# Cross-attention and a mixture of experts: how layer-normed tokens are transposed in front of the experts

## The chip, the cores and the metric

The kernel runs on one core of a Trainium2 chip. The metric is the device time of one execution in microseconds, lower is better. The kernel before takes 726.56 us (median of 3 runs, 726.43 to 727.07).

## The reference

All in f32. 1600 tokens (16 batches of 100) of width 256 pass a cross-attention over 361 context rows each and then a feed-forward stage with one shared and seven switched experts:

```python
def xattn(x, y, Wq, Wkv, Wproj, bproj):            # 16 heads of 64
    q = heads(x @ Wq); k, v = heads(y @ Wkv)
    a = softmax(q @ k.T * 64 ** -0.5) @ v
    return merge(a) @ Wproj + bproj

def swiglu(h, w1, w2, w3):                          # 256 -> 704 -> 256
    return silu(h @ w1.T) * (h @ w3.T) @ w2.T

def ffn(x, ...):
    probs = sigmoid(clip(x @ router_w.T + routing_bias, -50, 50))
    p, sel = top_k(probs, 1)
    y = swiglu of expert sel, times p
    total = clip(0.5 + p + 1e-8, 0.5, 2.0)
    return 0.5 / total * swiglu(x, shared) + y / total

x = x + xattn(layernorm(x), ctx, ...)
x = x + ffn(layernorm(x), ...)
```

## The kernel before

Tokens lie in 13 tiles of 128 (the last has 64). `acc` holds the residual stream, 128 tokens of a tile on the partitions; `xT` holds the normalised tokens turned round, features on the partitions (two halves of 128, index k), tokens along the free dimension, for use as the moving operand of TensorE. Four `GROUPS` of tiles, (0-2), (3-5), (6-8), (9-12), are handled together.

**Attention loop.** 32 steps `s`, two per batch (eight heads each). In each step, TensorE computes scores (L628) in pairs of heads, and between them the next key or value products (L561). VectorE finds the row maxima (L641), ScalarE takes exponentials (L644), and VectorE transposes the result in blocks of 32 into `tb` (L657). `moved` (L668) then puts the blocks in their places with 16 transfers into `aT`, eight issued by SP and eight by GpSimd, after a small transfer `row` and before two transfers `over` on SP. At the even steps `values` (L690) multiplies aT of the batch before with its values (L699). Two `tb` and two `aT` exist, so each is written again two steps on.

**Layer norm.** `layer_norm` (L161) returns a list of parts, `moments` per tile, `roots`, `normalise` per tile, and `turn`, which transposes the normalised tiles `xn` on TensorE against an identity, two tiles into one PSUM bank (L203), and copies the bank to `xT` on ScalarE (L206). With `keep=True` it is the norm in front of the experts: `normalise` also writes `xn` to DRAM (`xn_d`, L192), from where the experts gather tokens. The same function without `keep` is the norm in front of the attention. In the loop, `normalised` (L735) puts the parts into a queue `norms`, of which `part()` takes one behind most score units; once they are used up, `turned` is queued and runs at the next even step, and after it the router (`router`, L226, whose products at L235 read `xT`). So groups 0, 1 and 2 are normalised for the experts about steps 10 to 14, 18 to 22 and 26 to 30.

**Loads.** `load_later` (L150) issues, at the end of a step, what later steps need. Steps 10 to 15 call `load_shared` (L214): 10 to 13 load the four parts of the shared expert's first weights `w13_sb`, 14 the first three of the six row blocks of `w2_sb` (L220), 15 the other three by two transfers (L223, L224).

**Behind the loop.** The last step already computes the first hidden units of the shared expert for group 0 (`hidden`, L403, products at L412). Then come `down(GROUPS[0][:2])`, the first use of `w2_sb` (products at L455), the values of the last batch, `down` of the group's third tile, and the last projections (L726), which complete `acc`. Then:

```python
parts, turn_last = layer_norm(GROUPS[-1], keep=True)
for one in parts: one()
hT = run_hidden(GROUPS[1])
turn_last()
down(GROUPS[1][:1], hT)
for one in router(GROUPS[-1]): one()
down(GROUPS[1][1:], hT[:, :, P:])
fill = sort_tokens(hs)
```

`sort_tokens` gives the expert of each of up to 19 slots of 128 tokens; `fetch` (L881) has SP load an expert's weights by that number, and `gather_into` (L897) has GpSimd gather tokens. The other hidden and down products of the shared expert and then the slots follow.

**Order.** TensorE's order is the order of the text in the whole kernel. In the attention part, up to the last projection, the same holds for ScalarE, VectorE and SP; a scheduler places GpSimd's instructions, and behind the attention those of all engines but TensorE. Each DMA queue issues in its own order, and an issue that waits holds up those behind it. Waits between engines are semaphores that the framework puts in where tiles overlap.

Of the kernel before, what the change touches and what calls it, by code (L numbers as in the profile page):

```python
# [14 lines left out]
F32 = mybir.dt.float32  # L15
# [7 lines left out]
B, LQ, C = 16, 100, 256  # L23
# [3 lines left out]
P = 128  # L27
N = B * LQ
NT = (N + P - 1) // P
LAST = N - (NT - 1) * P  # L30
# [10 lines left out]
GROUPS = ((0, 1, 2), (3, 4, 5), (6, 7, 8), (9, 10, 11, 12))  # L41
# [13 lines left out]
def xattn_moe(  # L55
# [16 lines left out]
    nc = tc.nc  # L72

    def rows(t):
        return P if t < NT - 1 else LAST
# [9 lines left out]
    xT = const.tile([P, 2, NT * P], F32, name="xT")  # L85
# [24 lines left out]
    w2_sb = const.tile([P, NI + 1, C], F32, name="w2_sb")  # L110
# [4 lines left out]
    def bank():  # L115
        return ps.tile([P, 512], F32, tag="mm", name="mm")
# [10 lines left out]
    def load_x(g):  # L127
        full = [t for t in g if t < NT - 1]
        t0, n = full[0], len(full)
        nc.sync.dma_start(  # L130
            acc[:, t0 : t0 + n, :],
            x[t0 * P : (t0 + n) * P, :].rearrange("(t p) c -> p t c", p=P),
        )
        if g[-1] == NT - 1:
            nc.sync.dma_start(acc[:LAST, NT - 1, :], x[(NT - 1) * P :, :])
# [22 lines left out]

    biases = deque()

    def layer_norm(tiles, keep=False):  # L161


        n = len(tiles)
        of, xns = {}, []

        def moments(i):
            if i == 0:
                of["mv"] = small.tile([P, 4, 2], F32, name="mv")
                of["rstd"] = small.tile([P, 4], F32, name="rstd")  # L170
            st = small.tile([P, 6], F32, name="st")
            nc.vector.bn_stats(st, acc[:, tiles[i], :])
            nc.vector.bn_aggr(of["mv"][:, i, :], st)

        def roots():
            rstd = of["rstd"]
            nc.vector.tensor_scalar(rstd[:, :n], of["mv"][:, :n, 1], EPS, None, ALU.add)
            nc.gpsimd.tensor_tensor(rstd[:, :n], rstd[:, :n], power[:, :n], ALU.pow)

        def normalise(i):  # L180
            t = tiles[i]
            xn = small.tile([P, C], F32, name="xn", bufs=4)
            nc.vector.tensor_scalar(
                xn,
                acc[:, t, :],
                of["mv"][:, i, 0:1],
                of["rstd"][:, i : i + 1],
                ALU.subtract,
                ALU.mult,
            )  # L190
            if keep:
                nc.sync.dma_start(xn_d[t * P : t * P + rows(t), :], xn[: rows(t), :])  # L192
            else:
                biases.append(t)
            xns.append(xn)

        def turn():
            for i in range(0, n, 2):
                tr = bank()
                m = min(2, n - i)  # L200
                for o in range(m):
                    for k in range(2):
                        nc.tensor.transpose(  # L203
                            tr[:, ds((k * m + o) * P, P)], xns[i + o][:, ts(k, P)], ident
                        )
                nc.scalar.copy(  # L206
                    xT[:, :, ds(tiles[i] * P, m * P)],
                    tr[:, : 2 * m * P].rearrange("p (k n) -> p k n", k=2),
                )

        parts = [lambda i=i: moments(i) for i in range(n)] + [roots]
        return parts + [lambda i=i: normalise(i) for i in range(n)], turn

    def load_shared(i):  # L214

        if i < 4:
            k, o = i // 2, ds(i % 2 * I, I)
            nc.sync.dma_start(w13_sb[:, k, o], w13[ts(k, P), o])
        elif i == 4:
            nc.sync.dma_start(w2_sb[:, :3, :], w2[: 3 * P].rearrange("(i p) c -> p i c", p=P))  # L220
        else:
            r = w2[3 * P : NI * P].rearrange("(i p) c -> p i c", p=P)
            nc.sync.dma_start(w2_sb[:, 3:NI, :], r)  # L223
            nc.sync.dma_start(w2_sb[P - HALF :, NI, :], w2[NI * P :])  # L224
# [178 lines left out]
    def hidden(g, hT, sp, width=NB, same_table=0):  # L403


        n = sum(map(rows, g))

        nc.gpsimd.memset(hT[: P - HALF, NI, :n], 0.0)

        def product(to, at):  # L410
            for k in range(2):
                nc.tensor.matmul(  # L412
                    to[:, :n],
                    w13_sb[:, k, ds(at, P)],
                    xT[:, k, ds(g[0] * P, n)],
                    start=(k == 0),
                    stop=(k == 1),
                )

        def whole(i):  # L420
            pa, pb = bank(), bank()
            product(pa, i * P)
            product(pb, I + HALF + i * P)
            s = sp.tile([P, width], F32, name="s")
            if i < same_table:
                nc.scalar.activation(s[:, :n], pa[:, :n], AF.Tanh, scale=0.5)
                nc.vector.scalar_tensor_tensor(
                    s[:, :n], s[:, :n], 1.0, pa[:, :n], ALU.add, ALU.mult
                )
                nc.vector.scalar_tensor_tensor(  # L430
                    hT[:, i, :n], s[:, :n], 0.5, pb[:, :n], ALU.mult, ALU.mult
                )
                return
            nc.scalar.activation(s[:, :n], pa[:, :n], AF.Silu)
            nc.vector.tensor_tensor(hT[:, i, :n], pb[:, :n], s[:, :n], ALU.mult)

        def rest():

            pa = bank()
            product(pa, NI * P)  # L440
            s = sp.tile([P, width], F32, name="s")
            nc.scalar.activation(s[P - HALF :, :n], pa[:HALF, :n], AF.Silu)
            nc.vector.tensor_tensor(
                hT[P - HALF :, NI, :n], pa[P - HALF :, :n], s[P - HALF :, :n], ALU.mult
            )

        return [lambda i=i: whole(i) for i in range(NI)] + [rest]
# [16 lines left out]
    with ExitStack() as attn:  # L464
# [33 lines left out]
        def load_later(s):  # L498

            if 1 < s < 4:  # L500
                m = ts(s - 2, NCH // 2)
                nc.sync.dma_start(
                    wp_sb[:, m], wproj.rearrange("(m p) c -> p m c", p=P)[:, m]
                )
            if s == 3:
                nc.sync.dma_start(rb_sb, rbias.to_broadcast([P, E]))
                nc.sync.dma_start(rw_sb[:, :, :E], rwT.rearrange("(k p) e -> p k e", p=P))
            if s == 4 or s == 7:
                load_x(GROUPS[s // 3 + 1])
            if s == 6 or s == 9:  # L510
                normalised(GROUPS[s // 3])
            if 10 <= s < 16:
                load_shared(s - 10)

        NA = 4
        ats, qT_bufs = [], []
# [216 lines left out]
        turns, fillers, norms = deque(), deque(), deque()  # L733

        def normalised(g, keep=False):  # L735
            parts, turn = layer_norm(g, keep)
            norms.extend(parts)


            def turned():  # L740
                turn()
                if keep:
                    fillers.append(lambda: norms.extend(router(g)))

            norms.append(lambda: turns.append(turned))
# [34 lines left out]
        parts, turn_first = layer_norm(FIRST)  # L780
# [127 lines left out]
    with tc.tile_pool(name="hs", bufs=1) as hs:  # L908
        def run_hidden(g):
            n = sum(map(rows, g))  # L910
            hT = hs.tile([P, NI + 1, n], F32, name=f"hT{n}")
            for piece in hidden(g, hT, sp):
                piece()
            return hT

        parts, turn_last = layer_norm(GROUPS[-1], keep=True)
        for one in parts:
            one()
        hT = run_hidden(GROUPS[1])
        turn_last()  # L920
        down(GROUPS[1][:1], hT)
        for one in router(GROUPS[-1]):
            one()
        down(GROUPS[1][1:], hT[:, :, P:])
        fill = sort_tokens(hs)
        for k in range(NW):
            fetch(k)
        hT2 = run_hidden(GROUPS[2])
        fill()
        for k in range(NX - 1):  # L930
            gather_into(xgs, xn_d, k)
        hT3 = run_hidden(GROUPS[3])
        down(GROUPS[2], hT2)
        down(GROUPS[3], hT3)
    hp = ctx.enter_context(tc.tile_pool(name="hp", bufs=2))

    def turn(k):
        tr = bank()
        for j in range(2):
            nc.tensor.transpose(tr[:, ts(j, P)], xgs[k % NX][:, ts(j, P)], ident)  # L940
        xgT = xp.tile([P, 2, P], F32, name="xgT")
        nc.scalar.copy(xgT.rearrange("p k n -> p (k n)"), tr[:, : 2 * P])  # L942
        return xgT
# [63 lines left out]
    n = nc.values_load(e_at[:, NS:], min_val=0, max_val=NS - NF)  # L1007
# [58 lines left out]
```

## Time and profile before

| what | us |
|---|---|
| median of 3 runs | 726.56 |
| lowest, highest | 726.43, 727.07 |
| the profiled execution's own time | 726.04 |
| its span, first to last instruction | 724.3 |
| busy: TensorE, VectorE, ScalarE, GpSimd | 715.0, 420.7, 282.4, 198.7 |

Times in the profile are us from the span's start. Views used: busy time of each engine; instructions in order of time, equal neighbours merged (start, length, engine, line, operation, out<-in, shape, count; in brackets the idle time before and what ended it); groups of instructions by line (count, total us, mean ns of one); busy time by stretch. PE is TensorE (PEld its weight loads), DVE VectorE, ACT ScalarE, POOL GpSimd, SPq SP's queue of DMA issues. An f32 matrix product appears as two passes; a transpose as one. Names have their digits left out.

### The profile page before, as it was taken

How to read it: one execution, taken by the hardware profiler on the slowest of the kernel's cores; microseconds unless marked ns; L12 is line 12 of the kernel's file. 1: busy time of each engine (PE TensorE's matmuls, PEld its weight loads, DVE VectorE, ACT ScalarE, POOL GpSimd, SP SyncE). 2: the span in 40 equal slices, each digit the busy share in tenths (PEclk: the TensorE clock that was granted, in tenths of full speed). 3: DMA queues.
4: the chain of work that ended last, by engine and by line, in shares of the span. 5: the costliest groups of instructions: out<-in, count | busy, mean ns of one | idle time of the engine just before them, and what ended most of it. 6: DMA issues, size and time to landing. Idle time of an engine off the chain costs nothing. (4 is left out here: it accounts for less than half of the span.)

```text
span 724.3 us, 14799 instructions
## 1 busy us (share of the span) xinstructions
PE 715.0 (99%) x5216; PEld 515.0 (71%) x5216; DVE 420.7 (58%) x1090; ACT 282.4 (39%) x795; POOL 198.7 (27%) x419
## 2 busy tenths in 40 slices
PE   9999999999999999999999999999999999999996
PEld 6567667667566766757667576656866588999996
DVE  2777766867687676776777678677247221222221
ACT  2464563634546354463644636453021101112111
POOL 4242322322342222422224222233020103444221
PEclk9999999999999999999999999999999999999999
DMA  7156646444484643536435363444103901899860
GB/s 258 29 130 157 166 129 158 88 139 117 106 208 123 173 134 86 159 85 179 102 101 157 84 162 95 128 112 122 45 25 144 390 30 55 318 344 334 309 256 23
DMA packets 54375, 107.95 MB, mean 149 GB/s; under 512 B 28631, under 2 KB 35930, under 8 KB 52368
## 3 DMA queue, kind: packets, MB, share of 16 engines
q1 hardware_dynamic: 43648, 80.51, 36.3%
q0 software_dynamic: 10352, 25.98, 13.4%
q8 instruction: 44, 0.72, 0.4%
q14 instruction: 43, 0.35, 0.2%
q10 hardware_dynamic: 288, 0.39, 0.1%
HBM read 60.39 MB, written 5.35 MB: 91 GB/s over the span
## 5 line engine op out<-in xcount | busy, mean ns | idle before, releaser
L644 ACT ACTIVATE at<-mm,nm 128x361 f32<-128x361 f32 x256 | 141.6, 559 | 171.0 <-DVE nm L641 171.0
L678 POOL DMA_DIRECT2D aT<-tb x256 | 126.1, 500 | 296.7 <-PE mm L699 95.4
L641 DVE TENSOR_REDUCE nm<-mm 128x1 f32<-128x361 f32 x256 | 123.5, 523 | 61.7 <-PE mm L628 60.9
L657 DVE STREAM_TRANSPOSE tb<-at 128x384 f32<-128x384 f32 x256 | 133.0, 558 | 4.7
L561 PE MATMUL mm<-wv_sb,cT 64*128 64x512 f32 (+1 forms) x576 | 132.9, 589 | 0.8 <-ACT at L644 0.8
L561 PE MATMUL mm<-cT,wk_sb 64*128 64x361 f32 x768 | 126.5, 465 | 0.4 <-DMA cT<-in_ctxT 0.3
L561 PEld LDWEIGHTS mm<-cT,wk_sb 64*128 64x128 f32 x768 | 76.1, 188 | 45.7 <-issue 4.2
L628 PE MATMUL mm<-kT,qT 64*128 64x361 f32 x512 | 98.2, 474 | 0.0
L561 PEld LDWEIGHTS mm<-wv_sb,cT 64*128 64x128 f32 (+1 forms) x576 | 55.7, 181 | 57.2 <-issue 44.5
L949 PE MATMUL mm<-xgT,wex 128*128 128x128 f32 x660 | 78.3, 275 | 0.5 <-ACT xgT L942 0.5
L949 PEld LDWEIGHTS mm<-xgT,wex 128*128 128x128 f32 x660 | 76.9, 192 | 1.4 <-issue 0.7
L699 PE MATMUL mm<-aT,v 128*64 128x100 f32 (+1 forms) x1536 | 72.7, 251 | 0.8 <-DMA over<-row 0.4
L699 PEld LDWEIGHTS mm<-aT,v 128*64 128x64 f32 (+1 forms) x1536 | 69.3, 135 | 5.0 <-issue 3.0
L628 PEld LDWEIGHTS mm<-kT,qT 64*128 64x128 f32 x512 | 48.3, 186 | 34.2 <-issue 8.2
L412 PE MATMUL mm<-xT,w_sb 128*128 128x384 f32 (+1 forms) x176 | 60.9, 503 | 0.0
L412 PEld LDWEIGHTS mm<-xT,w_sb 128*128 128x128 f32 x176 | 32.9, 190 | 26.1 <-issue 8.5
L644 ACT ACTIVATION_READ_ACCUMULATOR at<-mm,nm 128x1 f32 x256 | 50.4, 197 | 0.0
L726 PE MATMUL mm<-wp_sb,resT 128*128 128x256 f32 (+1 forms) x208 | 48.0, 384 | 0.0
L537 PE MATMUL mm<-xT,wq_sb 128*128 128x200 f32 x256 | 46.9, 336 | 0.0
L537 PEld LDWEIGHTS mm<-xT,wq_sb 128*128 128x128 f32 x256 | 43.4, 190 | 4.0 <-issue 2.0
L726 PEld LDWEIGHTS mm<-wp_sb,resT 128*128 128x128 f32 (+1 forms) x208 | 37.8, 186 | 11.2 <-issue 4.4
L591 ACT COPY kT<-mm 128x361 f32<-128x361 f32 x64 | 29.4, 460 | 41.6 <-PE mm L561 41.6
(141 smaller groups left out, 553.6 us busy)
## 6 DMA issues: line engine op xcount, KB each, us to landing
wex<-in_wex SPq DMA_DIRECT2D x15, 2176.0 KB
aT<-tb POOLq DMA_DIRECT2D x256, 80.2 KB, 3.0
aT<-tb SPq DMA_DIRECT2D x256, 80.2 KB
cT<-in_ctxT SPq DMA_DIRECT2D x15, 541.5 KB
over<-row SPq DMA_DIRECT2D x64, 100.0 KB
xn_d<-xn SPq DMA_DIRECT2D x12, 128.0 KB
base_d<-acc SPq DMA_DIRECT2D x12, 128.0 KB
w_sb<-in_w SPq DMA_DIRECT2D x4, 352.0 KB
```

Source lines behind the costliest of these rows:

```text
L412: nc.tensor.matmul(to[:, :n], w13_sb[:, k, ds(at, P)], xT[:, k, ds(g[0] * P, n)], start=(k == 0), stop=(k == 1),)
L537: nc.tensor.matmul(pq[:, o, :], wq_sb[:, u, k, ts(o, P)], xT[:, k, ts(g, QG * LQ)], start=(k == 0), stop=(k == 1),)
L561: nc.tensor.matmul(to[o][:height, :width], *operands(o, k), start=(k == 0), stop=(k == NR - 1),)
L591: nc.scalar.copy(kT[:, c, :], to[0][:, :LKV])
L628: nc.tensor.matmul(sc[o][:, :LKV], qTs[b // QG][r, c, ts(b % QG, QB), :], kTs[b][c // 4][r, c % 4, :], start=True, stop=True,)
L641: nc.vector.tensor_reduce(nm[:, o : o + 1], sc[o][:, :LKV], AX.X, ALU.max, negate=True)
L644: nc.scalar.activation(at[:, o, :LKV], sc[o][:, :LKV], AF.Exp, bias=nm[:, o : o + 1], accum_out=sums[:, o : o + 1],)
L657: nc.vector.transpose(tb[:, :, :, o, i * QR : i * QR + 32].rearrange("p j k n -> p k j n"), at[:, o, :].rearrange("p (k j n) -> p k j n", ...
L678: queue.dma_start(aT[ts(j, 32), i].rearrange("p k o n -> p (k o n)"), tb[ts(i, 32), j].rearrange("p k o n -> p (k o n)"),)
L699: nc.tensor.matmul(av[ts(o, DK), i, :], vs[b][:n, j, ds((2 * c + o) * DK, DK)], aT[:n, :, j, o, ts(i, QR)], start=(j == 0), stop=(j == NJ ...
L726: nc.tensor.matmul(pp[:r, :C], resT[:, c, QP : QP + r], wp_sb[:, c, :], start=(c == 0), stop=(c == NCH - 1))
L949: nc.tensor.matmul(to[:, ts(o, P)], w[:, ds(j * 2 * I + u, P)], xgT[:, j, :], start=(j == 0), stop=(j == 1),)
```

## The change

In front of the experts, VectorE transposes each normalised tile in blocks of 32 into a block buffer, straight behind its normalisation. Two new parts of the list, `move(k)`, put the blocks of feature half k in their places in `xT` with 16 transfers each, eight on SP's queue and eight on GpSimd's; `turn` returns at once. The norm in front of the attention is as before. For groups 0 to 2 the block buffer is the memory of the first four row blocks of `w2_sb`, and so the loads of w2 go from steps 14 and 15 to steps 30 and 31, the last two; for the last group it is a tile of its own, `blocks`.

```diff
-    def layer_norm(tiles, keep=False):
+    def layer_norm(tiles, blocks=None):
         n = len(tiles)
         of, xns = {}, []
+        keep = blocks is not None
+        full = sum(t < NT - 1 for t in tiles)
+        if keep:
+            xb = blocks.rearrange("p (c n) -> p c n", c=8)[:, :, : n * 32]
...
             if keep:
                 nc.sync.dma_start(xn_d[t * P : t * P + rows(t), :], xn[: rows(t), :])
+                nc.vector.transpose(xb[:, :, ts(i, 32)], xn.rearrange("p (c n) -> p c n", n=32))
             else:
                 biases.append(t)
             xns.append(xn)
 
+        def move(k):
+            for q in range(4):
+                for c in range(4):
+                    queue = nc.gpsimd if (q + c) % 2 else nc.sync
+                    m = n if q * 32 < LAST else full
+                    to = xT[ts(c, 32), k, ds(tiles[0] * P, m * P)]
+                    of = xb[ts(q, 32), 4 * k + c, : m * 32].rearrange("p (i n) -> p i n", n=32)
+                    queue.dma_start(to.rearrange("p (i n) -> p i n", n=P)[:, :, ts(q, 32)], of)
+
         def turn():
+            if keep:
+                return
             for i in range(0, n, 2):
...
-        return parts + [lambda i=i: normalise(i) for i in range(n)], turn
+        parts += [lambda i=i: normalise(i) for i in range(n)]
+        if keep:
+            parts += [lambda k=k: move(k) for k in range(2)]
+        return parts, turn
...
-            if 10 <= s < 16:
+            if 10 <= s < 14:
                 load_shared(s - 10)
+            if s >= 2 * B - 2:
+                load_shared(s - 2 * B + 6)
...
         def normalised(g, keep=False):
-            parts, turn = layer_norm(g, keep)
+            parts, turn = layer_norm(g, w2_sb.rearrange("p c n -> p (c n)")[:, : 8 * P] if keep else None)
             norms.extend(parts)
...
-        parts, turn_last = layer_norm(GROUPS[-1], keep=True)
+        blocks = hs.tile([P, 8 * P], F32, name="blocks")
+        parts, turn_last = layer_norm(GROUPS[-1], blocks)
         for one in parts:
             one()
         hT = run_hidden(GROUPS[1])
```

## The prediction, made before the changed kernel was run

> **What bounds the kernel now.** I read the table of busy times first, then TensorE's order of time around each place that the diff touches, then the queues there.
>
> ```profile
> PE 715.0 (99%) x5216; PEld 515.0 (71%) x5216; DVE 420.7 (58%) x1090; ACT 282.4 (39%) x795; POOL 198.7 (27%) x419
> ```
>
> TensorE is busy 715.0 of 724.3 us and its order is written out by hand, so a wait in it moves the end by its own length. VectorE, GpSimd and the DMA have idle time; new work there costs only where it makes TensorE wait. The next view (TensorE in order of time: start, us, line, what, number of passes) shows a turn inside the attention loop, and then the stretch behind it.
>
> ```profile
> 256.87 0.88 PE L203 MATMUL mm<-ident,xn 128*128 128x128 f32 x6
> 257.67 0.88 PE L628 MATMUL mm<-kT,qT 64*128 64x361 f32 x4
> ...
> 502.32 3.62 PE L726 MATMUL mm<-wp_sb,resT 128*128 128x256 f32 x16
> 505.78 5.34 PE L455 MATMUL mm<-w_sb,v 128*128 128x256 f32 x24
> 511.05 4.52 PE L699 MATMUL mm<-aT,v 128*64 128x100 f32 x96
> ...
> 539.63 1.04 PE L203 MATMUL mm<-ident,xn 128*128 128x128 f32 x8
> 540.50 2.76 PE L455 MATMUL mm<-w_sb,hT 128*128 128x256 f32 x12
> 543.19 0.64 PE L235 MATMUL mm<-xT,rw_sb 128*32 128x128 f32 x16
> ```
>
> Starts are what counts: six transposes take 257.67 - 256.87 = 0.80 us, eight take 540.50 - 539.63 = 0.87. The first product with w2 stands at 505.78, the last router at 543.19. (The profile drops digits: w_sb is w13_sb or w2_sb; at L455, w2_sb.)
>
> **The change, part by part.**
>
> *TensorE and ScalarE lose work.* 26 transposes go: 6 in each of three turns in the loop, 8 in the last. In the loop that is 3 x 0.80 = 2.4 us off TensorE, which I count in full; from 0 (if something else sets the pace there) to 5.0 (if the two copies of each turn, 0.88 us of ScalarE by its order of time, counted too). The last turn's 0.87 us is in the sum below.
>
> *VectorE gains 13 transposes of 128x256.* The rows are 558 ns for 128x384 (L657) and 320 ns for 128x128 (L244); between them about 0.44 us. In the loop that is three times 0.44 per group, one per unit of score work, where VectorE shows idle gaps of 0.3 to 1.8 us within some units; nothing on the path (if that cover were gone, up to 1.3 us a group). In the last group they come straight behind the normalisation.
>
> *128 transfers are added, 32 a group,* half from SP, half from GpSimd, each of 32 partitions with 3 or 4 pieces of 128 B. What does one cost to issue?
>
> ```profile
> L678 POOL DMA_DIRECT2D aT<-tb x256 | 126.1, 500 | 296.7 <-PE mm L699 95.4 <-DVE nm L641 42.1 <-PE mm L203 41.1
> L899 POOL DMA_INDIRECT xg<-xn_d,slot_token x15 | 15.2, 1016 | 25.0 <-DMA wex<-in_wex 17.7 <-PE mm L949 2.5 <-issue 2.1
> ```
>
> GpSimd takes 500 ns (column behind the comma) for 32 pieces, 1016 ns for the gather's 128. SP's queue has 8 aT issues in 5.02 us, 0.628 each, and 0.633 for the over transfers of 256 pieces: on SP the number of pieces doesn't matter. (On both queues a transfer waits until the eighth before it has landed; eight issues, 4.0 us or more, cover aT's 3.0.) On GpSimd the Trainium skill (DMA: Bandwidth & Descriptors, "Anatomy of one DMA — SWDGE (gpsimd) path") says that many descriptors can be emitted before the cost shows; that would leave it at 0.5. The two rows differ by 516 ns for 96 more pieces, 5.4 ns a piece, though the gather also reads an index. I take the rows, as the gather's count of pieces is the one that is nearest: 0.85 for 96 pieces, 1.02 for 128; the ends are 0.5 and the gathers' start-to-start of 1.4.
>
> *In the loop* the sixteen of each queue stand ahead of that step's eight aT issues. Group 0: the last normalised tile is written out at 236.09, blocks ready about 237. GpSimd: 16 x 0.85 = 13.6, so its aT issues move from 240.0 to 250.6 and land about 257.6. SP: 16 x 0.63 = 10, row, aT and over end at 254.6 instead of 247.1; SP's next step begins at 257.66. The aT is read at 269.9 (L699), and its source tb is rewritten two steps on, after 260. So nothing is late. The router that reads xT stands at 266.5. With 1.4 us an issue the landing would pass 264, VectorE would wait for tb, and TensorE for VectorE: 0 to 2 us a group. Taken: 0.
>
> *The load of w2 moves from steps 14 and 15 to 30 and 31,* since the blocks use its memory. Its second part (256 and 64 KB) now stands in SP's queue behind the last step's transfers:
>
> ```profile
> 501.45 5.47 SPq L678 DMA_DIRECT2D aT<-tb  x8
> 506.97 1.29 SPq L684 DMA_DIRECT2D over<-row  x2
> 509.08 10.14 SPq L461 DMA_DIRECT2D base_d<-acc  x3
> ```
>
> These are SP's issues in order of time (the aT, over and base_d of the last step). The load can be issued at 508.3 at the earliest. But the product at 505.78 needs it from its fourth row block on: 24 passes in 5.27 us are 0.44 us a block, so at 507.1. The nearest row is the first w2 load of today's kernel, which also follows two over transfers (SP's order of time; below it busy time by stretch, whose last two columns are DMA share and GB/s):
>
> ```profile
> 247.19 0.60 SPq L220 DMA_DIRECT2D w_sb<-in_w  x1
> ```
> ```profile
> 250.00:250.50 0.50, 0.50 (x6) 0.33 (x4) 0.27 (x1) 0.12 (x1) 0.00 (x0) 1.00 0.80 281
> 250.50:251.00 0.50, 0.50 (x6) 0.34 (x4) 0.00 (x0) 0.00 (x0) 0.00 (x0) 1.00 0.04 14
> ```
>
> Traffic falls from 281 to 14 GB/s at 250.5, 3.3 us behind the issue. That gives 508.3 + 3.0 = 511.3 for 256 KB and a **stall of 4.2 us** (511.3 - 507.1); 3.2 to 5.1 with the 2.0 and 3.9 us that aT takes at least and at most to land. Behind it in TensorE's order stand the last step's values (L699), whose aT has long landed, then projection, last layer norm, everything. No other engine uses the time. The first part, issued about 491.8, lands before 496.
>
> *The last group.* Normalised tiles are there at
>
> ```profile
> 529.26 1.86 DVE L183 TENSOR_SCALAR xn<-acc,mv,rstd 128x256 f32<-128x256 f32 x4 [1.15 <-POOL rstd L178]
> ```
>
> 531.1; the four transposes stand in between (two behind each pair), so blocks are ready at 531.1 + 4 x 0.44 = 532.9. SP has issued its four xn_d writes by then: 15 x 0.628 more to the start of its last transfer, 542.4. GpSimd: eight of 1.02 and eight of 0.85 are 14.9, the last starts at 547.0. Landing takes
>
> ```profile
> DMA to landing us min/median/max: 2.0/3.0/3.9
> ```
>
> 3.0 (the aT transfers), so xT is whole at 545.4 by SP, at **550.0 by GpSimd**. TensorE comes to the router at 543.19 - 0.87 = 542.3 and waits 7.7 us; net of the 0.87 the rest moves by 550.0 - 543.2 = **6.8 us**. By the skill's rule GpSimd is done at 533 + 15 x 0.5 + 3 = 543.5 and SP sets it: 2.2 us. Below: landing in 2.0 us, 1.2. Above: 1.4 us an issue and the gathers' 5.8 us to land, 16.6. Behind the router wait: rest of the down product, the router's chain on VectorE, the sort, the expert numbers that SP's expert weight loads wait for, and the gathers; all shift alike, so the order behind is not further disturbed.
>
> *A clock that may fall.* The same skill (TensorE: Matmul & The Clock Gate, "What's actually happening") says that after about 3.4 us of idleness TensorE runs at half its clock until it has been busy as long. Here the granted clock is 1.00 throughout and no wait is over 1.1 us, though the twelve first passes (L122) take 0.24 us each where L949's of the same size take 0.11. By that rule the router wait costs 1.7 us more, the w2 wait (4.2) up to as much; by the trace nothing. I put 0 in the sum and 3.4 in the range.
>
> **Sum.** -2.4 (loop) + 4.2 (w2) + 6.8 (last group) = +8.6. The profiled execution took 726.04 (span 724.3): 734.6. The median of the runs shown is 0.5 above it: **735.1 us**.
>
> **Rivals.**
> *A flat price on GpSimd* (the skill's rule): -2.4 + 4.2 + 2.2 = +4.0, 730.6. For it: SP's price doesn't grow with pieces either, and the gather reads indices. Against it: the 500 and 1016 above.
> *Dearer transfers or a cold clock*: pieces of 128 B slower to land, loop transfers late for tb, TensorE at half clock after the waits: 739 to 748. For it: 3584 pieces in the last group are 224 for each of 16 engines; against it, over's 400 B pieces go at 100 GB/s at 0.59 share (508.5 to 509.0), some 38 ns each, so 224 are 8.5 us, inside the 14.9.
> *Not slower: the loop gives back more.* Place: the turns between a step's products, where transposes and ScalarE copies hold two PSUM banks and delay exponentials (ScalarE waits 171.0 us for VectorE at L644). It decides from 2.1 us a group if GpSimd is flat (losses 4.2 + 2.2), 3.7 us by my rows. The most I can read is 1.7 us a group (0.80 + 0.88), with transfers landing in 2.0 us: -5.0 + 3.2 + 1.2 = -0.6, 726.0.
>
> **How the numbers follow.** Mine 0.5, flat price 0.28, dearer 0.12, not slower 0.10 (half of it faster by over 0.2%). 0.2%, 1.5 us, is about what a measurement here tells from no change. Mine alone: 733 to 738. The range, 729 to 741, takes in the flat price and the lower end of the dear case and leaves out the third rival. Slower 0.90, same 0.05, faster 0.05.
>
> **What would show it.** At L455 TensorE should wait some 4 us for a DMA into w2 inside the first tile, and some 7 us at the router for one into xT; GpSimd's xT issues should read 0.85 to 1.0 us. If they read 0.5, the flat rival holds and the router wait is near 3. If aT reads or VectorE's tb writes wait in steps 14 to 16, 22 to 24 or 28 to 30, the loop's cover was misjudged. The prediction falls if either wait is missing, or if the loop ends over 3 us earlier.

## The result, and the profile after

The kernel after takes 732.81 us (median of 6 runs, 731.95 to 734.86), the kernel before, run beside it on the same chip, 727.02 (6 runs, 726.43 to 728.36). The ratio is 1.0081, 95% interval 1.0065 to 1.0096: 5.8 us slower. The profiled execution of the kernel after took 733.04 us, its span is 731.3.

Busy time by engine, kernel after (busy us, share of the span, instructions):

```profile
PE 714.4 (98%) x5190; PEld 514.5 (70%) x5190; DVE 425.2 (58%) x1103; ACT 279.0 (38%) x787; POOL 234.2 (32%) x483
```

TensorE has 26 instructions fewer, but only 0.6 us less of busy time, and the span is 7.0 us longer. So it must be waiting longer than before, or working more slowly, somewhere. First the loop, where it was to gain. TensorE in order of time, at the values of the batch before the first turn, between the turns, and behind the third (start, us, line, what, passes; in brackets the wait and what ended it), kernel after:

```profile
236.86 4.51 PE L721 MATMUL mm<-aT,v 128*64 128x100 f32 x96
268.41 4.51 PE L721 MATMUL mm<-aT,v 128*64 128x100 f32 x96
358.48 4.51 PE L721 MATMUL mm<-aT,v 128*64 128x100 f32 x96
476.57 4.49 PE L721 MATMUL mm<-aT,v 128*64 128x100 f32 x96 [0.33 <-ACT at L666]
```

and the same four in the kernel before:

```profile
237.35 4.52 PE L699 MATMUL mm<-aT,v 128*64 128x100 f32 x96
269.90 4.52 PE L699 MATMUL mm<-aT,v 128*64 128x100 f32 x96
360.60 4.51 PE L699 MATMUL mm<-aT,v 128*64 128x100 f32 x96
479.76 4.51 PE L699 MATMUL mm<-aT,v 128*64 128x100 f32 x96 [0.37 <-DMA aT<-tb]
```

The kernel after leads by 0.49 us ahead of the first turn, then by 1.49, 2.12 and 3.19. Of the first lead, 0.48 is there one batch earlier (204.14 against 204.62), before anything that was changed has run: this is how two executions differ. The three turns give 3.19 - 0.49 = 2.7 us. None of these value products waits longer than it did. Then the stretch behind the loop, TensorE again, kernel after:

```profile
502.56 1.46 PE L475 MATMUL mm<-w_sb,v 128*128 128x256 f32 x6
509.02 6.05 PE L475 MATMUL mm<-w_sb,v 128*128 128x256 f32 x18 [5.00 <-DMA w_sb<-in_w]
515.00 4.49 PE L721 MATMUL mm<-aT,v 128*64 128x100 f32 x96
...
543.55 2.75 PE L475 MATMUL mm<-w_sb,hT 128*128 128x256 f32 x12
546.24 0.63 PE L255 MATMUL mm<-xT,rw_sb 128*32 128x128 f32 x12
547.37 0.38 PE L255 MATMUL mm<-xT,rw_sb 128*32 128x128 f32 x2 [0.51 <-DMA xT<-blocks]
548.58 0.38 PE L255 MATMUL mm<-xT,rw_sb 128*32 128x128 f32 x2 [0.82 <-DMA xT<-blocks]
548.89 5.45 PE L475 MATMUL mm<-w_sb,hT 128*128 128x256 f32 x24
```

The first line with w2 (L475, the old L455) now stops after 6 of 24 passes and waits 5.00 us for w2. From its start to the values behind it are 515.00 - 502.56 = 12.44 us, where before it was 511.05 - 505.78 = 5.27: 7.2 us more. In the last group, the router waits 0.51 and 0.82 us between its passes; from the start of one down product to the next are 548.89 - 543.55 = 5.34 us. Before, from the eight transposes at 539.63 through the product to its second part, it was 543.76 - 539.63 = 4.13: 1.2 us more. The line of that second part, kernel before:

```profile
543.76 5.45 PE L455 MATMUL mm<-w_sb,hT 128*128 128x256 f32 x24
```

The rest of the 7.2 us, beyond the wait, is in the granted clock. Busy time by stretch, kernel after (stretch, length, busy time of PE, PEld, DVE, ACT, POOL with instructions, then granted clock, DMA share, GB/s):

```profile
504.00:506.00 2.00, 0.02 (x1) 0.00 (x0) 0.00 (x0) 0.00 (x0) 0.00 (x0) 1.00 0.38 92
506.00:508.00 2.00, 0.00 (x0) 0.00 (x0) 0.00 (x0) 0.00 (x0) 0.00 (x0) 0.53 0.91 220
508.00:510.00 2.00, 0.98 (x2) 0.84 (x3) 0.00 (x0) 0.00 (x0) 0.00 (x0) 0.50 0.06 17
510.00:512.00 2.00, 2.00 (x6) 1.64 (x5) 0.04 (x1) 0.00 (x0) 0.00 (x0) 0.50 0.03 8
512.00:514.00 2.00, 2.00 (x8) 1.66 (x8) 0.45 (x1) 0.00 (x0) 0.00 (x0) 0.77 0.20 66
514.00:516.00 2.00, 2.00 (x27) 1.59 (x28) 0.48 (x1) 0.00 (x0) 0.00 (x0) 1.00 0.00 0
```

TensorE stops at 504.0; at about 506.1 its clock falls to 0.50 and stays there until about 513, four microseconds into the work that the weights release. The 18 passes behind the wait take 515.00 - 509.02 = 5.98 us, at the old pace (5.27/24 each) 3.95: about 2.0 us lost to the clock. Why w2 was late is in SP's queue, kernel after (start, us from first issue to end of the last, line, transfer, count):

```profile
498.30 5.43 SPq L700 DMA_DIRECT2D aT<-tb  x8
503.78 1.29 SPq L706 DMA_DIRECT2D over<-row  x2
505.12 0.60 SPq L243 DMA_DIRECT2D w_sb<-in_w  x1
...
536.78 10.34 SPq L210 DMA_DIRECT2D xT<-blocks  x16
```

The second load of w2 is issued at 505.12, right behind `over`, and its weights are there at 509.02, 3.9 us later. GpSimd's share of the block transfers and the gather that it was priced by, by group (line, transfer, count, busy us, mean ns of one, then idle time before), kernel after:

```profile
L700 POOL DMA_DIRECT2D aT<-tb x256 | 126.6, 502 | 252.9 <-PE mm L721 68.4 <-DVE nm L663 49.7 <-issue 38.7
L210 POOL DMA_DIRECT2D xT<-w_sb x48 | 26.0, 549 | 14.7 <-issue 12.1 <-DMA xT<-w_sb 2.5
L922 POOL DMA_INDIRECT xg<-xn_d,slot_token x15 | 15.2, 1016 | 25.8 <-DMA wex<-in_wex 17.7 <-PE mm L973 3.5 <-DMA xT<-blocks 2.1
L210 POOL DMA_DIRECT2D xT<-blocks x16 | 8.8, 556 | 3.2 <-DVE blocks L198 2.4 <-issue 0.8
```

A block transfer of 96 pieces costs GpSimd 549 ns, and those of the last group, 96 and 128, cost 556. The issues by operation in the last group (shortest, median, longest ns; first and last start), kernel after:

```profile
L210 POOL DMA_DIRECT2D xT<-blocks x16: 547/551/611, 536.4 to 545.4; - x16
L210 SPq DMA_DIRECT2D xT<-blocks x16: 597/599/662, 536.8 to 546.5; - x16
L198 DVE STREAM_TRANSPOSE blocks<-xn x4: 397/415/434, 534.3 to 536.0; 128x256 f32<-128x256 f32 x4
...
DMA to landing us min/median/max: 1.7/1.7/1.8
```

GpSimd starts its last transfer at 545.4, SP at 546.5: SP's queue ends the group. GpSimd's transfers land in 1.7 us; the landings of SP's are not recorded, but the router's last passes start 2.1 us after SP's last transfer.

By the traces, then: loop -2.7, w2 +7.2, last group +1.2, and -0.5 that was there beforehand: +5.1 at the start of the sort (554.17 against 549.05). The end of these two profiled executions is 7.0 apart. Of the rest, 1.0 us lies in the slots, where the changed code has no part, and 0.9 behind the start of the last product.

Most of these 0.9 us belong to the change. GpSimd ends the program with an instruction named DRAIN, which the views above leave out but the traces hold. It takes 0.97 us in the three kernels whose GpSimd issues what it issued before (the kernel before, experiments 2 and 7 below), 1.61 in the four that add all 64 of its block transfers (the kernel after, experiments 1, 5 and 6), and 2.1 to 2.2 in the three that add 48, 16 or 13 transfers (experiments 3, 4 and 8). From the start of the last product to the end of the span, the three sets take 10.8 to 11.0, 11.5 to 11.7 and 12.1 to 12.2 us. So more transfers on GpSimd's queue go with 0.6 us more at the very end here, and with 1.2 in experiments 3 and 4. That is read from one trace of each kernel; why the DRAIN grows, and not in step with their number, is not shown.

### The profile page after: what moved, and what is told of

Its sections match the earlier page's. It is cut to its first block, busy times and chain, and to the rows that moved or that the text cites. A ratio compares the mean times of both kernels' runs of the same rounds, so it can differ in the third digit from the quotient of the medians.

```text
span 731.3 us, 14960 instructions
## 1 busy us (share of the span) xinstructions
PE 714.4 (98%) x5190; PEld 514.5 (70%) x5190; DVE 425.2 (58%) x1103; ACT 279.0 (38%) x787; POOL 234.2 (32%) x483
```

## The experiments

My theory: nearly the whole loss is w2's second load, which the borrowed memory pushes behind the last step's transfers, and the loop really gives its 2 to 3 us. The rivals left were that the last group or the transfers in the loop cost as much, or that the gain in the loop is no gain of the transposes. The first four kernels separate the three parts; the others settle the clock, the router wait, VectorE's part and GpSimd's price. Experiments 1 to 4 ran on one chip and 5 to 7 on another (the kernel before: 726.04 and 727.16), so ratios are compared.

**1. The kernel after, but with both loads of w2 in step 30.**

```diff
-            if s >= 2 * B - 2:
-                load_shared(s - 2 * B + 6)
+            if s == 2 * B - 2:
+                load_shared(4)
+                load_shared(5)
```

> Both loads of w2 at the end of step 30, all else as changed. Theory (the second load at step 31 costs a wait of 5.0 us and then half clock, 7.2 us in all from the first down product to the values behind it): the wait disappears, this stretch takes 5.3 us again, and the time falls by 7.2 to about 725.6, below the kernel before. Rival (something else would have been waited for there anyway, the last step's aT and over transfers or the values): the stretch still takes over 9 us and the time stays above 730.

Measured: 725.45 against 726.04, ratio 0.999 (0.9982 to 0.9999). TensorE in order of time:

```profile
503.63 5.34 PE L475 MATMUL mm<-w_sb,v 128*128 128x256 f32 x24
508.90 4.51 PE L722 MATMUL mm<-aT,v 128*64 128x100 f32 x96
...
541.25 0.38 PE L255 MATMUL mm<-xT,rw_sb 128*32 128x128 f32 x2 [0.46 <-DMA xT<-blocks]
542.47 0.38 PE L255 MATMUL mm<-xT,rw_sb 128*32 128x128 f32 x2 [0.83 <-DMA xT<-blocks]
```

The stretch is 508.90 - 503.63 = 5.27 us again, as before the change, with no wait. The router's two waits are untouched. Moving one load by one step turns 5.8 us slower into slightly faster (0.1 to 1.3 us).

**2. The kernel before, but with the loads of w2 in steps 30 and 31 and nothing else.**

```diff
-            if 10 <= s < 16:
+            if 10 <= s < 14:
                 load_shared(s - 10)
+            if s >= 2 * B - 2:
+                load_shared(s - 2 * B + 6)
```

> The kernel before, with nothing changed but that w2 is loaded at steps 30 and 31. Theory: one wait of about 5 us at the fourth pass pair of the first down product, half clock behind it, +7.2 us, about 734.2. Rival (the wait is long in the changed kernel only because the transfers of blocks and the block memory delay the loads): under 2 us slower than before.

Measured: 734.08 against 726.04, ratio 1.0109 (1.0093 to 1.0125), 8.0 us slower. TensorE in order of time:

```profile
505.62 1.46 PE L455 MATMUL mm<-w_sb,v 128*128 128x256 f32 x6
512.12 6.58 PE L455 MATMUL mm<-w_sb,v 128*128 128x256 f32 x18 [5.05 <-DMA w_sb<-in_w]
518.63 4.48 PE L701 MATMUL mm<-aT,v 128*64 128x100 f32 x96
```

The stretch is 13.01 us, 7.7 more than before: 5.05 of wait, and 18 passes in 6.51 us, 2.6 more than their old 3.95, as the granted clock is 0.50 from about 510.3 to 517. So the late load makes the loss by itself, with no block transpose in the kernel.

**3. Experiment 1, with the last group turned by TensorE as before: the loop's part alone.**

```diff
-        blocks = hs.tile([P, 8 * P], F32, name="blocks")
-        parts, turn_last = layer_norm(GROUPS[-1], blocks)
+        parts, turn_last = layer_norm(GROUPS[-1], store=True)
```

(`store` writes `xn_d` and leaves `turn` as it was.)

> Groups 0 to 2 by VectorE, the last group by TensorE as before, w2 loaded at step 30. Theory (terms add: loop -2.7, last group +1.2, w2 +7.2): only the loop's part is left, 727.0 - 2.7 = 724.3, 1.3 below the kernel with both w2 loads at step 30. Rival (the loop gives nothing and the earlier start of the down product in the trace is chance of that execution): 727.

Measured: 724.25 against 726.04, ratio 0.9976 (0.9967 to 0.9986): 1.8 us faster (1.0 to 2.4), less than the forecast 2.7. In its trace, the values ahead of the first turn and behind the third stand at 237.29 and 477.01 where the kernel before has 237.35 and 479.76: 2.7 us, as in the kernel after. In all ten traces this stretch takes 242.4 to 242.5 us in the five kernels whose loop turns on TensorE and 239.7 to 239.9 in the five in which VectorE and the block transfers take its place, so the loop's gain is real. Part of it is missing at the end, where GpSimd's DRAIN is 1.2 us longer than before.

**4. The kernel before, with the last group alone turned by VectorE** (w2 loaded in steps 14 and 15; `layer_norm` is the changed one, and groups 0 to 2 use its `store`).

```diff
-        parts, turn_last = layer_norm(GROUPS[-1], keep=True)
+        blocks = hs.tile([P, 8 * P], F32, name="blocks")
+        parts, turn_last = layer_norm(GROUPS[-1], blocks)
```

> The kernel before, with only the last group by VectorE; w2 at steps 14 and 15. Theory: a router wait of about 2 us less 0.87 for the transposes, +1.2, about 728.2. Rival (the forecast's price of 0.85 to 1.02 us an issue on GpSimd, which the earlier stall hid): +6.8, about 733.8.

Measured: 728.14 against 726.04, ratio 1.0029 (1.0017 to 1.0042), 2.1 us slower. TensorE in order of time:

```profile
539.45 2.75 PE L477 MATMUL mm<-w_sb,hT 128*128 128x256 f32 x12
542.13 0.63 PE L257 MATMUL mm<-xT,rw_sb 128*32 128x128 f32 x12
543.06 0.38 PE L257 MATMUL mm<-xT,rw_sb 128*32 128x128 f32 x2 [0.29 <-DMA xT<-blocks]
544.46 0.38 PE L257 MATMUL mm<-xT,rw_sb 128*32 128x128 f32 x2 [1.03 <-DMA xT<-blocks]
544.77 5.45 PE L477 MATMUL mm<-w_sb,hT 128*128 128x256 f32 x24
```

From one down product to the next are 5.32 us, 1.2 more than before, and GpSimd's DRAIN is 1.2 longer: 2.4 together, where the medians show 2.1 (1.2 to 3.0). The last group costs between one and three microseconds, not seven.

The medians of the parts, -1.8, +8.0 and +2.1, make +8.3, and the whole is +5.8. The DRAIN explains most of the difference: its cost is in experiments 3 and 4 with 1.2 us each, but in the whole only once, with 0.6. With it, the traces give -2.7 + 1.2 = -1.5 for experiment 3, +7.7 for experiment 2, +2.4 for experiment 4 and -2.7 + 7.2 + 1.2 + 0.6 = +6.3 for the kernel after. Each lies within the interval of its ratio; for the whole that is 4.7 to 7.0.

**5. The kernel after, with 18 products of ones by ones, whose result nothing reads, ahead of the first down product.** It keeps the load late, but TensorE busy.

```diff
+        idle = bank()
+        for _ in range(18):
+            nc.tensor.matmul(idle[:, :P], ones, ones, start=True, stop=True)
         down(GROUPS[0][:2], hT0)
```

> The changed kernel with 18 products of ones by ones on TensorE ahead of the first down product (about 4.1 us of work that nobody reads). Theory (the wait for w2 lets TensorE's clock fall, which costs about 2 us behind it): the products fit into the wait, the clock stays whole, and the time falls by 2.0 against the changed kernel, to about 731. Rival (the passes behind the wait are slow for another reason, or the clock costs nothing in the end): the same as the changed kernel or slower by up to 4 us.

Measured: 731.31 against 727.16, ratio 1.0062 (1.0048 to 1.0075). TensorE in order of time:

```profile
502.57 4.18 PE L887 MATMUL mm<-ones 128*128 128x128 f32 x36
506.59 1.46 PE L475 MATMUL mm<-w_sb,v 128*128 128x256 f32 x6
508.67 4.12 PE L475 MATMUL mm<-w_sb,v 128*128 128x256 f32 x18 [0.62 <-DMA w_sb<-in_w]
512.72 4.48 PE L721 MATMUL mm<-aT,v 128*64 128x100 f32 x96
```

And busy time by stretch of the same kernel, where the clock had been 0.50:

```profile
510.00:512.00 2.00, 2.00 (x11) 1.74 (x11) 0.48 (x1) 0.00 (x0) 0.00 (x0) 1.00 0.18 62
```

The clock stays at 1.00, the 18 passes take 512.72 - 508.67 = 4.05 us instead of 5.98, and the whole stretch 10.15 instead of 12.44. The idleness makes the low clock, and its price is 5.98 - 4.05 = 1.9 us; the other 0.35 us of the stretch is that the weights came earlier here (508.67 against 509.02). The times agree in sign (+4.5 us by the ratio, against +5.8), but their intervals overlap; the trace decides this one.

**6. Experiment 1, with one unit of the next hidden product ahead of the last router.**

```diff
         down(GROUPS[1][:1], hT)
+        hT2 = hs.tile([P, NI + 1, 3 * P], F32, name="hT2")
+        units = hidden(GROUPS[2], hT2, sp)
+        units.pop(0)()
         for one in router(GROUPS[-1]):
             one()
...
-        hT2 = run_hidden(GROUPS[2])
+        for piece in units:
+            piece()
```

> Both w2 loads at step 30, and one hidden unit of group 2 (2.6 us of TensorE) moved ahead of the last router. Theory (SP's sixteen issues of 0.65 us set the router's wait of about 2 us, and only that wait makes the last group dearer by VectorE than by TensorE): the wait is gone and the time is 2 us under the kernel with both loads at step 30, 723.4 to 723.6. Rival (the router only waits for what comes later as well, the sort's chain on VectorE): the wait reappears in front of the sort and the time stays at 725.5.

Measured: 724.16 against 727.16, ratio 0.9963 (0.995 to 0.9977), 2.7 us faster than the kernel before by the ratio. TensorE in order of time:

```profile
539.21 2.74 PE L432 MATMUL mm<-xT,w_sb 128*128 128x384 f32 x8
541.88 0.65 PE L255 MATMUL mm<-xT,rw_sb 128*32 128x128 f32 x16
542.46 5.45 PE L475 MATMUL mm<-w_sb,hT 128*128 128x256 f32 x24
```

Eight passes, 2.7 us of work that has to be done anyway, stand where the waits were, and the router runs in one piece. Experiment 1 was 0.7 us faster than the kernel before by its ratio, so covering the router brings 2.0, as forecast. With w2's load and the router covered, the change is a gain. Whether the kernel before would gain from the same reordering was not run; its router waits for nothing.

**7. The kernel before, with VectorE's nine block transposes of the loop added and their result read by nothing, and both loads of w2 in step 30.** TensorE turns every tile as before.

```diff
+                nc.vector.transpose(xb[:, :, ts(i, 32)], xn.rearrange("p (c n) -> p c n", n=32))
...
-            if 10 <= s < 16:
+            if 10 <= s < 14:
                 load_shared(s - 10)
+            if s == 2 * B - 2:
+                load_shared(4)
+                load_shared(5)
```

> TensorE turns all groups as before; VectorE makes the nine block transposes of groups 0 to 2 as well, which nobody reads; no added transfers; w2 at step 30. Theory (VectorE's transposes in the loop and the later w2 loads are hidden): the time of the kernel before. Rival (VectorE's 0.44 us reaches TensorE): up to 9 x 0.44 = 4.0 us slower.

Measured: 726.83 against 727.16, ratio 0.9995 (0.9987 to 1.0003). VectorE's transposes cost nothing in the loop, and w2 loaded at 30 costs nothing either.

**8. What does GpSimd pay for 128 pieces?** In the kernel before, the writes of `xn_d` (128 partitions, one piece of 1 KB each) go to GpSimd's queue.

```diff
-                nc.sync.dma_start(xn_d[t * P : t * P + rows(t), :], xn[: rows(t), :])
+                nc.gpsimd.dma_start(xn_d[t * P : t * P + rows(t), :], xn[: rows(t), :])
```

> The kernel before, with the normalised tiles written to DRAM by transfers that GpSimd issues instead of SP: 128 partitions of 1 KB each, plain transfers. Theory (pieces are nearly free on GpSimd, and the gathers' 1.0 us is for reading the index): the issue reads 0.5 to 0.6 us. Rival (the price goes with the number of partitions or rows, and is low for the block transfers because they have 32 partitions): 0.9 to 1.0 us. The time is not the question.

Measured, GpSimd's groups by line as above:

```profile
L899 POOL DMA_INDIRECT xg<-xn_d,slot_token x15 | 15.2, 1014 | 24.6 <-DVE slot_token L397 17.7 <-DMA xn_d<-xn 2.4 <-issue 2.1
...
L192 POOL DMA_DIRECT2D xn_d<-xn x13 | 7.4, 568 | 7.1 <-DVE at L654 3.0 <-DVE xn L183 1.9 <-issue 1.7
```

128 rows by plain addresses cost 568 ns, 128 rows by index 1014 ns, in the same kernel. The gather's second half microsecond is not for the number of its pieces; it goes with the indexed form. Nor is it the direction: the indexed writes of the results (out_x, L966) cost 1020 ns in this trace. The kernel's own time (729.75 in its only run) wasn't the question here.

## Why the prediction was right, and where its steps were not

Sign and size held: 732.81 lies in the range, 2.3 us below the predicted 735.1; as a change, +5.8 against a forecast of +8.6. That closeness is partly luck. Two of the three terms were wrong, in opposite directions: the last group's came out 5.6 us lower, w2's with its clock 3.0 us higher. The rival of the flat price, 730.6, is as near from below. Of the signs that the prediction named, the wait for w2 came (5.0 us where it said some 4); a router wait of some 7 us and an issue price of 0.85 to 1.0 did not. They were 1.3 and 0.55, and by the prediction's own words that is the rival's sign.

*"In the loop that is 3 x 0.80 = 2.4 us off TensorE, which I count in full."* Right: 2.7 us by the trace. The third rival needed more than 4.4 us here even with its lowest costs (3.2 + 1.2). The loop gave 0.3 us more than the transposes' own 2.4, so it leaves little room for the ScalarE copies on the path.

*VectorE's transposes at about 0.44 us, hidden.* Right: 445 ns in the loop, 415 in the last group, and experiment 7 finds no cost.

*"So nothing is late" in the loop.* Right: the value products in the lines above start no later for aT than they did. The working was off, though. "Written out at 236.09" is when SP's queue came to that tile; VectorE had normalised it by 232.3, and in the kernel after GpSimd starts to move blocks at 232.94. Its aT issues then begin at 243.93, not at 250.6, at 0.55 us for each block transfer and with two waits of 0.61 and 1.46 us until earlier block transfers had landed.

*"That gives 508.3 + 3.0 = 511.3 for 256 KB and a stall of 4.2 us."* The mechanism of the wait was right in every link: the queue, the place behind `over`, the fourth row block. With the loop's 3.2 us lead taken off, I had forecast the issue at 505.1, and it came at 505.12. The 3.0 us for landing were too short: 3.9 here and 3.85 in experiment 2. I had set it by aT's median, below the 3.3 us at which the bandwidth falls in an earlier load; the range's upper end, 5.1, was the right one. The term measured 5.0.

*"I put 0 in the sum and 3.4 in the range"* for the clock. This step failed: the end moves by more than the wait's length. "Here the granted clock is 1.00 throughout" was a misreading. Among TensorE's products no wait was longer than 1.1 us, so there the trace of before could show no fall of the clock. But TensorE's last product ends at 718.8, and 3.3 us later the clock falls, kernel before:

```profile
722.00:724.00 2.00, 0.00 (x0) 0.00 (x0) 0.00 (x0) 0.00 (x0) 0.00 (x0) 0.52 0.04 8
```

For the wait of 4 us, the prediction's estimate by the Trainium skill's rule (TensorE: Matmul & The Clock Gate, "What's actually happening") was up to 1.7 us. Measured: 2.0 us in the kernel after, 1.9 by experiment 5. The clock fell sooner than after the rule's 3.4 us of idleness: 2.1 us after the last product in the kernel after, 3.2 in experiment 2. The two router waits, of 0.5 and 0.8 us with work between them, leave the clock alone: the 24 passes behind them take 5.45 us, no longer than experiment 6's without a wait.

*"I take the rows, as the gather's count of pieces is the one that is nearest: 0.85 for 96 pieces, 1.02 for 128."* This is the step that failed most: 6.8 us forecast for the last group, 1.2 measured. The two rows differ in number of pieces and in kind, and I put the whole difference down to the number. The prediction names the other cause ("though the gather also reads an index") and then passes over it. Experiment 8 shows that the kind decides. With the flat price GpSimd ends before SP, and SP's sixteen issues set the router's wait, just as the rival of the flat price has it: it gives 2.2 us for this term, 1.0 too much (1.2 with the landing in 2.0 us that the prediction names as its lower end). I had SP's last transfer start at 542.4 and land at 545.4. Measured from the down product ahead (3.92 us later in this trace, 543.55 against 539.63), it started at 546.5 - 3.92 = 542.6, and the router's last passes began at 548.58 - 3.92 = 544.7: 2.1 us later, where I had taken aT's 3.0. The other 0.3 us is that only the router's last two passes had to wait for the last blocks, not its first.

So the rival's last group and my w2 term, with the clock and GpSimd's DRAIN that neither sum counted, make the result: -2.7 + 5.0 + 2.0 + 1.2 + 0.6 = 6.1 us, beside 5.8 measured.

## What to carry to other kernels

When a change borrows memory, the loads that owned that memory move too. Look up where each now stands in its queue and when its first reader runs: here one load at the end of a queue cost 7 us where the loop gained 2.7, and issuing it a step earlier got it back. Price an issue by a row of the same kind of transfer, not of the same count, and remember that a wait of several microseconds on TensorE costs its own length and then the clock behind it.

## What was not expected of the hardware

- TensorE's granted clock fell to 0.50 about 2.1 us after the last product (504.0 to some 506.1), in experiment 2 after 3.2 us (507.1 to 510.3), and was back at 1.00 only four to five microseconds after work began again (509.02 to 513, 512.12 to 517). It was low for 6.8 us both times. A wait of 5.0 us cost 7.2 and 7.7.
- GpSimd's price for issuing a plain transfer hardly depends on its shape: 502 ns for aT's 32 pieces, 549 for 96 and 556 for 96 to 128 pieces of 128 B, 568 for 128 pieces of 1 KB. The indexed form with 128 rows costs 1014 to 1026.
- In the last group, GpSimd's block transfers, all in the chip's own memory, landed within 1.7 to 1.8 us although they consist of 96 or 128 pieces of 128 B; aT's larger ones take 2.0 to 3.9 in the kernel before. In the loop such transfers took 1.6 to 6.1 us; what held them up there was not tested.
